# Second attention, first pass: the row maxima marked as high priority for VectorE's queue

## Chip, cores and metric

One NeuronCore of a Trainium2 chip. The metric is device microseconds for one execution of the whole program. The kernel before was timed three times: median 3221.76 us (3221.34 to 3221.77). One further execution was recorded by the hardware profiler.

## What is computed

The input x has 16 sequences of 512 tokens by 128 channels. Two gated layers follow each other, each of the form x + s(xn) * silu(g(xn)), with xn the layer norm of x. In the first, s is a gated causal convolution and g a two-layer transformer with local attention (8 heads of 64, windows of 64). In the second, s is attention over the whole sequence (16 heads of 8 channels) and g a soft mixture of experts. The change sits in the second layer's attention:

```
q = apply_rope(proj(Wq, bq), rope)
k = apply_rope(proj(Wk, bk), rope)
scores = jnp.einsum('bhqd,bhkd->bhqk', q, k) / math.sqrt(hd)
probs = jax.nn.softmax(scores, axis=-1)
out = jnp.einsum('bhqk,bhkd->bhqd', probs, v)
```

## The kernel before

**Stages.** The body is a set of Python generators, each of which emits the instructions of one stage for one of the 16 sequences ("batches"): C the convolution and P the setup (once each), L0 and L0b the two transformer layers (`layer`), A the start of the second layer (`pre`: gate, norm, q, k and v, rope, transposes), S1 and S2 the two passes of the second attention (`first`, `second`), M the mixture of experts (`moe`). A heap merges the generators: every `yield` tells how much work was just emitted, and PLAN gives each stage a start and a length in units of batches, so that some eight stages of several batches are emitted interleaved.

**Order of the queues.** That emission order is not yet the order of the instructions. It gives each instruction a priority, and Tile's scheduler, which plays the program through with times of its own, gives each engine in turn the instruction of best priority among those it holds ready. What comes out is one fixed list for each engine. In the trace an engine starts its instructions in that order, and stands idle when the next one lacks an input or a free buffer. `tc.high_priority()` puts the instructions traced inside it ahead of all others in this choice; the existing `tied` helper uses it to keep groups of matmuls together.

**S1 (`first`, L566 to L597).** For each batch there are four groups `G_` of four heads. A group loads packed queries QS and keys KS (three sets in turn, DMAs at L575 and L576), and then does 16 steps, four query tiles `qt` by four heads `g`:

```
sc = pt_("s1", "s1")
PE.matmul(sc, QS[:, g // 2, qt * 128 : qt * 128 + 128], KS[:, g % 2, :], start=True, stop=True)
V.tensor_reduce(mx[:, g, qt : qt + 1], sc, AX.X, ALU.max)
yield 0.7
```

So one step is a score matmul on TensorE (L583, tile s1c, one PSUM bank) and a maximum over its 512 keys on VectorE (L584, into one column of tile mw). There are 16 x 4 x 16 = 1024 steps, 64 to a batch. The tag s1 owns one PSUM bank, so the matmul of a step can start only when the maximum of the step before has read the bank; for the last two batches `TAIL` lets it use a second bank. After 16 steps mw is transposed (L587, tile pmc), negated and split (L589, L590), stored (L593) and written into spare rows of QS (L595), so that the second pass gets scores with the maximum already subtracted.

**S2 (`second`).** For each group 16 matmuls (L618, tile s2d, one bank), each followed by an exponential on ScalarE (L620); after each second key tile 8 matmuls with the values (L602, tile pvd), at the end a copy and four transposes. `turned` releases the QS and KS set.

**Others that this text names.** In `layer`: the projection into bank pq (L221 to L223 for the three parts of one product) is read by ScalarE (L335, L336) and by VectorE (L337, L341), then a sum of squares (L348, VectorE) and the normalisation on GpSimd; the scores of the local attention (L379) are masked and their minima taken on VectorE (L392, eight pairs of instructions to a window group), exponentials on ScalarE (L396), transposes (qT, kT, prT; they all carry L209), values (L123, L126), 1/sum and product (L414, L415), output projection (L433). In `moe`: logits (plb, also L221 to L223) with a maximum (L723), puob (L731, read at L732, L733, L736). At the end of `second`: the gate and residual (L657 to L662).

Of the kernel before, what the change touches and what calls it, by code (L numbers as in the profile page):

```python
# [13 lines left out]
ALU = mybir.AluOpType  # L14
AX = mybir.AxisListType
# [82 lines left out]
def body(ctx, tc, a):  # L98
    nc = tc.nc
    NB = a["x"].shape[0]  # L100
    V, S, G, PE = nc.vector, nc.scalar, nc.gpsimd, nc.tensor
# [90 lines left out]
    def mk(sid, b, dflt):  # L192
        def tl(shape, tag, dt=F32):
            cnt[0] += 1
            tg = f"{tag}{sid}"
            return pools[sid].tile(shape, dt, tag=tg, name=f"{tag}{sid}_{b}_{cnt[0]}", bufs=NBUF.get(tg, 2))

        def pt_(nm, tag=dflt):
            cnt[0] += 1
            alt = TAIL.get((tag, NB - b))  # L200
            if alt:
                turns_[tag] = turns_.get(tag, 0) + 1
                tag = alt[turns_[tag] % len(alt)]
            return psb.tile([128, 512], F32, tag=TAGS[tag], name=f"{nm}{sid}_{b}_{cnt[0]}", bufs=NPSUM[TAGS[tag]])

        def quad(src, nm, tag=dflt):
            pt = pt_(nm, tag)
            for p in range(4):
                PE.transpose(pt[:, p * 128 : p * 128 + 128], src(p), ident)  # L209
            return pt  # L210

        def split(pt, tag):
            t = tl([128, 2, 512], tag, F32R)
            S.copy(t[:, 0, :], pt)
            V.tensor_tensor(t[:, 1, :], pt, t[:, 0, :].bitcast(F32), ALU.subtract)  # L215
            return t

        return tl, pt_, quad, split
# [258 lines left out]
    def together(key, act, last=None):  # L477
        if key is None:
            act()
            return  # L480
        want = (0, 3)
        k = key[1]
        n = sum(0 <= k - o < NB for o in want)
        meet.setdefault(key, []).append((last is not None, act, last))
        if len(meet[key]) == n:
            todo = sorted(meet[key], key=lambda x: x[0])
            first = todo[0][1]()
            if todo[-1][2] is not None and len(todo) > 1:
                behind(first, todo[-1][2])
            tied([lambda: first] + [x[1] for x in todo[1:]])  # L490
            meet[key] = None
        while meet[key] is not None:
            yield 0.3
# [72 lines left out]
    def first(b):  # L566
        tl, pt_, quad, split = mk("c", b, "aS1")
        for G_ in range(4):
            n = 4 * b + G_
            assert turned[0] > n - len(ops)  # L570
            QS, KS = ops[n % len(ops)]
            qsrc = scq[b % 2, 128 * G_ : 128 * G_ + 128]
            ksrc = sck[b % 2, 128 * G_ : 128 * G_ + 128]
            for i in range(2):
                dma(out=QS[64 * i : 64 * i + 64, i, :].bitcast(F32), in_=qsrc[64 * i : 64 * i + 64].bitcast(F32))  # L575
                dma(out=KS[i:128:2, i, :].bitcast(F32), in_=ksrc[i:128:2].bitcast(F32))  # L576
            mw = maxima[n % 2]
            mx = mw[:, 0:16].rearrange("t (g q) -> t g q", g=4)
            yield 2
            for qt in range(4):  # L580
                for g in range(4):
                    sc = pt_("s1", "s1")
                    PE.matmul(sc, QS[:, g // 2, qt * 128 : qt * 128 + 128], KS[:, g % 2, :], start=True, stop=True)  # L583
                    V.tensor_reduce(mx[:, g, qt : qt + 1], sc, AX.X, ALU.max)  # L584
                    yield 0.7
            pm = pt_("pm")
            PE.transpose(pm[:80, 0:128], mw, ident)  # L587
            mm = tl([16, 2, 128], "mm", F32R)
            S.activation(mm[:, 0, :], pm[:16, 0:128], AF.Copy, scale=-1.0)  # L589
            V.scalar_tensor_tensor(mm[:, 1, :], pm[:16, 0:128], -1.0, mm[:, 0, :].bitcast(F32), ALU.mult, ALU.subtract)  # L590
            dst = mxd[b % 2, G_]
            for i in range(2):
                dma(out=dst[i].rearrange("j n t -> n j t").bitcast(F32), in_=mm[8 * i : 8 * i + 8].bitcast(F32))  # L593
            for i in range(2):
                dma(out=QS[64 * i + 48 : 64 * i + 52, i, :].bitcast(F32), in_=dst[i].rearrange("j (g q) t -> (j g) (q t)", g=2).bitcast(F32))  # L595
            qks[b, G_] = (QS, KS)
            yield 1  # L597
# [257 lines left out]
    def late():  # L855
# [81 lines left out]
    box, xrs, prs = {}, {}, {}  # L937
    make = {
        "L0": lambda b: layer(b, 0, box), "L0b": lambda b: layer(b, 1, box), "A": pre, "S1": first, "S2": second,
        "M": lambda b: moe(b, xrs, prs),  # L940
        "C": lambda b: conv(), "P": lambda b: setup(),
# [91 lines left out]
```

## Time and profile before

| | us |
|---|---|
| median of three runs | 3221.76 |
| profiled execution, its own time | 3220.23 |
| its span | 3218.4 |
| PE busy | 2932.7 (91%) |
| PEld busy | 2173.2 (68%) |
| DVE busy | 2334.5 (73%) |
| ACT busy | 2071.7 (64%) |
| POOL busy | 1596.0 (50%) |
| L584, 1024 maxima | 697.9 busy, 685 ns each |
| L583, 1024 score matmuls | 454.5 busy, 446 ns each |

PE is TensorE's matmuls, PEld its weight loads, which overlap them; DVE is VectorE, ACT ScalarE, POOL GpSimd and SP the engine that issues most DMAs. The span runs from the first to the last instruction of the profiled execution; 1.8 us of its time lie outside. A row of the waits says which instruction's engine stood idle, and which instruction's end let it go on, with the sum, the number of times and the longest. A row of the timeline gives the start in the span, the duration, the engine, the line, the operation and the tiles (out<-in), and in brackets the idle time before it. Line numbers are those of the kernel before; in the changed kernel the lines from the maximum on are one higher.

### The profile page before, as it was taken

The numbers are of one execution on the slowest core, as the hardware profiler recorded it, in microseconds if no ns is written. First come the engines' busy times: TensorE is split into PE (matmuls) and PEld (weight loads), VectorE is DVE, ScalarE is ACT, GpSimd is POOL, SyncE is SP. The second block draws the span as 40 slices with busy tenths as digits, with TensorE's granted clock in tenths as the row PEclk, the third lists the DMA queues.
The fourth block names the chain that finished last, engine by engine and source line by source line (L and its number), as shares of the span: only waits on it lengthen the run. The fifth ranks groups of instructions, "written<-read, shape, count | busy, mean of one in ns | idle before, by whom it ended". The sixth has DMA issues, their size and how long they took to land.

```text
span 3218.4 us, 67550 instructions
## 1 busy us (share of the span) xinstructions
PE 2932.7 (91%) x24164; PEld 2173.2 (68%) x24164; DVE 2334.5 (73%) x7165; ACT 2071.7 (64%) x4803; POOL 1596.0 (50%) x1854
## 2 busy tenths in 40 slices
PE   5798878889999999999999999999999999999897
PEld 4687756566767767676767677676767676666553
DVE  5779567768777877777787778777777778776563
ACT  2645445657766766676666667676766766656565
POOL 2424366655546473745556464747465564542200
PEclk7999979999999999999999999999999999999998
DMA  7555443122222222222222221221222222211110
GB/s 249 146 141 131 109 118 95 51 81 65 79 65 66 64 79 73 53 82 61 79 66 84 58 76 54 78 73 53 83 59 80 67 82 57 72 51 50 29 46 18
DMA packets 199549, 251.55 MB, mean 78 GB/s; under 512 B 57488, under 2 KB 123184, under 8 KB 199216
## 3 DMA queue, kind: packets, MB, share of 16 engines
q1 hardware_dynamic: 180784, 196.90, 21.4%
q0 software_dynamic: 18432, 50.34, 6.0%
q8 instruction: 193, 3.16, 0.4%
q14 instruction: 140, 1.15, 0.1%
HBM read 159.84 MB, written 57.50 MB: 68 GB/s over the span
## 4 chain that ended last, share of the span: by engine, by line
PE 57%; DVE 17%; ACT 13%; POOL 5%; issue 4%; DMA 3%; SPq 1%; POOLq 0%; DVEq 0%; ACTq 0%
PE pvd L602 7%; PE s2d L618 5%; PE s1c L583 5%; PE pw L433 3%; DVE mw L584 3%; ACT sd L620 3%; PE pw L471 3%; PE sc L379 2%; PE pq L221 2%; PE prT L209 2%; PE ppb L714 2%; DVE pr L392 2%; ACT pr L396 2%; PE pq L223 2%; PE pq L222 2%
## 5 line engine op out<-in xcount | busy, mean ns | idle before, releaser
L584 DVE TENSOR_REDUCE mw<-s1c 128x1 f32<-128x512 f32 x1024 | 697.9, 685 | 260.3 <-PE s1c L583 253.0
L620 ACT ACTIVATE sd<-s2d 128x512 f32<-128x512 f32 x1024 | 612.4, 603 | 331.5 <-PE s2d L618 325.2
L618 PE MATMUL s2d<-QS,KS 128*128 128x512 f32 x1024 | 479.6, 471 | 44.7 <-ACT sd L620 39.7
L583 PE MATMUL s1c<-KS,QS 128*128 128x512 f32 x1024 | 454.5, 446 | 51.8 <-DVE mw L584 43.5
L354 POOL TENSOR_TENSOR y<-ss,mhalf 128x8 f32<-128x8 f32 x256 | 429.6, 1678 | 15.6
L396 ACT ACTIVATE pr<-pr,m 128x128 f32<-128x128 f32 x1024 | 333.6, 396 | 107.9 <-DVE m L392 107.8
L352 POOL TENSOR_SCALAR ss<-ss 128x8 f32<-128x8 f32 x256 | 62.1, 242 | 641.8 <-DVE ss L348 621.7
L618 PEld LDWEIGHTS s2d<-QS,KS 128*128 128x128 f32 x1024 | 192.2, 188 | 237.7 <-issue 114.3
L350 POOL TENSOR_TENSOR rt<-rt,q 128x512 f32<-128x512 f32 x256 | 328.0, 1281 | 3.5 <-DVE q L341 3.5
L335 ACT ACTIVATE q<-pq 128x256 f32<-128x256 f32 x512 | 197.4, 385 | 143.7 <-PE pq L223 136.0
L355 POOL TENSOR_TENSOR rt<-rt,y 128x512 f32<-128x512 f32 x256 | 268.7, 1050 | 16.2
L583 PEld LDWEIGHTS s1c<-KS,QS 128*128 128x128 f32 x1024 | 193.6, 189 | 121.1 <-DVE mw L584 92.4
L337 DVE TENSOR_TENSOR rt<-pq,rot 128x256 f32<-128x256 f32 x512 | 212.4, 415 | 73.1 <-ACT vbuf L336 48.9
L602 PE MATMUL pvd<-sd,Vt 128*32 128x512 f32 x2048 | 249.2, 605 | 1.9 <-ACT sd L620 1.9
L221 PE MATMUL pq<-wq,hT 128*128 128x384 f32 x512 | 207.3, 405 | 25.1 <-DVE q L341 16.9
L341 DVE TENSOR_TENSOR q<-pq,rot 128x256 f32<-128x256 f32 x512 | 212.7, 415 | 0.0
L348 DVE TENSOR_REDUCE ss<-q 128x8 f32<-128x512 f32 x256 | 174.3, 681 | 50.8 <-ACT q L335 50.3
L209 PE MATMUL prT<-step,pr 128*128 128x128 f32 x1024 | 189.6, 281 | 15.3 <-ACT pr L396 10.5
L401 ACT COPY pt<-prT 128x512 f32<-128x512 f32 x256 | 152.3, 595 | 63.8 <-PE prT L209 61.1
L223 PE MATMUL pq<-wq,hT 128*128 128x384 f32 x512 | 178.6, 349 | 1.4 <-DVE hT L215 0.4
L323 POOL DMA_DIRECT2D wq<-wqd x128 | 81.4, 636 | 197.8 <-PE pq L223 140.4
L222 PE MATMUL pq<-wq,hT 128*128 128x384 f32 x512 | 178.8, 349 | 0.0
(255 smaller groups left out, 7435.9 us busy)
## 6 DMA issues: line engine op xcount, KB each, us to landing
wq<-wqd POOLq DMA_DIRECT2D x128, 384.0 KB, 3.7
w<-w1d SPq DMA_DIRECT2D x32, 682.0 KB
vsbuf<-vbuf SPq DMA_DIRECT2D x128, 130.0 KB
QS<-scq SPq DMA_DIRECT2D x128, 128.0 KB
KS<-sck SPq DMA_DIRECT2D x128, 128.0 KB
vsbuf<-vbuf SPq DMA_DIRECT2D x128, 97.5 KB
scq<-sa SPq DMA_DIRECT2D x96, 128.0 KB
sck<-sa SPq DMA_DIRECT2D x96, 128.0 KB
```

What stands on the lines that cost most here:

```text
L209: PE.transpose(pt[:, p * 128 : p * 128 + 128], src(p), ident)
L221: PE.matmul(out, lh, rh, start=start, stop=False)
L222: PE.matmul(out, lh, rl, start=False, stop=False)
L350: G.tensor_tensor(rf, rf, t2.rearrange("t p d -> t (p d)"), ALU.add)
L354: G.tensor_tensor(y.rearrange("t p g -> t (p g)"), sh, mhalf[:, 0:8], ALU.pow)
L355: G.tensor_tensor(rt[:, ps], rt[:, ps], y[:, :, :, None].to_broadcast([128, 2, 4, 64]), ALU.mult)
L396: S.activation(pr[:, hh, p, :], pr[:, hh, p, :], AF.Exp, bias=m[:, hh, p : p + 1], scale=-1.0)
L583: PE.matmul(sc, QS[:, g // 2, qt * 128 : qt * 128 + 128], KS[:, g % 2, :], start=True, stop=True)
L584: V.tensor_reduce(mx[:, g, qt : qt + 1], sc, AX.X, ALU.max)
L602: return PE.matmul(pv[32 * q : 32 * q + 32, :], Vt[:, kt, 9 * hd : 9 * hd + 32], e, start=(last == 1 and kt == 1), stop=(last == 3 and kt ...
L618: PE.matmul(sc, KS[:, g % 2, kt * 128 : kt * 128 + 128], QS[:, g // 2, :], start=True, stop=True)
L620: S.activation(e, sc, AF.Exp, scale=ISQ8)
```

## The change

The maximum of each step is traced inside `tc.high_priority()`. The matmul in front of it, the other stages, the buffers, PLAN and the yields are as they were.

```
                     PE.matmul(sc, QS[:, g // 2, qt * 128 : qt * 128 + 128], KS[:, g % 2, :], start=True, stop=True)
-                    V.tensor_reduce(mx[:, g, qt : qt + 1], sc, AX.X, ALU.max)
+                    with tc.high_priority():
+                        V.tensor_reduce(mx[:, g, qt : qt + 1], sc, AX.X, ALU.max)
                     yield 0.7
```

## Prediction

> **What bounds the kernel now.** I read the page's engine totals first, then the waits by engine, then the windows, then the timeline at the places where TensorE stops. The totals:
>
> ```profile
> PE 2932.7 (91%) x24164; PEld 2173.2 (68%) x24164; DVE 2334.5 (73%) x7165; ACT 2071.7 (64%) x4803; POOL 1596.0 (50%) x1854
> ```
>
> PE is busy for 2932.7 of 3218.4 us, so all its idle time is 285.7 us, and VectorE has 884 us to spare. The waits of PE over the whole span, then the top wait of VectorE:
>
> ```profile
> PE s1c L583 <- DVE mw L584: 43.5, 99, 1.6
> PE s2d L618 <- ACT sd L620: 39.7, 59, 2.7
> ...
> PE pq L221 <- DVE q L341: 16.9, 24, 4.5
> ```
>
> ```profile
> DVE mw L584 <- PE s1c L583: 253.0, 265, 3.9
> ```
>
> The change aims at the first row: a score matmul waits for the maximum before it to free the one bank. The row is 43.5 us, 1.4% of the span; that is the most the change can take away there. The last row says that 265 of the 1024 maxima had VectorE standing ready before their matmul ended: those can't come sooner by a better place in VectorE's queue.
>
> The windows tell the kernel's phases:
>
> ```profile
> 519.20:1252.70 733.50, 683.22 (x5847) 507.30 (x5848) 552.33 (x1768) 494.98 (x1172) 409.80 (x467) 0.99 0.25 71
> 1252.70:2662.90 1410.20, 1340.02 (x11297) 986.90 (x11296) 1077.56 (x3369) 981.16 (x2305) 781.12 (x897) 1.00 0.25 70
> 2662.90:3090.60 427.70, 393.08 (x2796) 268.30 (x2795) 292.00 (x805) 274.68 (x578) 159.66 (x196) 0.98 0.19 54
> 3090.60:3218.40 127.80, 107.80 (x558) 58.39 (x556) 55.04 (x113) 73.72 (x139) 9.93 (x13) 0.93 0.08 22
> ```
>
> The first PE figure is busy time. The second window is a steady state of eight batches: in the order of the queues each batch repeats the one before, instruction by instruction, every 176.3 us (1410.2 / 8). PE idles there for 70.2 us, 8.8 a batch. The waits of that window hold this row:
>
> ```profile
> PE s1c L583 <- DVE mw L584: 23.7, 56, 0.8
> ```
>
> 56 / 8 = 7 stalls a batch, always at the same steps, 2.96 us together. I number a batch's 64 steps from 0 and give, from the timeline (means of seven batches), the stall ahead of a step and, in brackets, how long the maximum of the step before had to wait after its matmul's end: 9: 0.37 (0.04), 23: 0.16 (0.55), 25: 0.36 (0.04), 33: 0.63 (2.18), 35: 0.24 (1.07), 48: 0.78 (0.04), 55: 0.42 (1.83). Three of them, 1.51 us, are pure latency: the maximum started 0.04 us after its matmul, took 0.69, and 0.05 later the next matmul ran. No order on VectorE helps these. The other four, 1.45 us a batch, stand behind other VectorE work: L348 (23), L662 (33), L392 (35 and 55).
>
> **The change, part by part.** It adds and removes no instruction: 1024 maxima at 685 ns remain. What moves is read from the orders of both programs side by side. *First*, in the steady state all of S1 moves ahead by two steps: the interval before step r + 2 now holds what the interval before step r held, for 50 of 64 intervals on PE and 51 of 64 on VectorE, identically. Without S1, 897 of 908 PE and 351 of 357 VectorE instructions of a batch keep their order. So the maxima don't leap out of VectorE's queue; they already were where the scheduler held them ready, and one place lets S1 squeeze in a step. I cost the shift by itself at nothing: the same PE work surrounds each of the seven stalls, which are now ahead of steps 11, 25, 27, 35, 37, 50 and 57. Step 33's maximum stays behind L662, and the L392 groups stay whole (111 unbroken runs before, 123 after). The transposes of mw (L587) and the DMAs to QS behind them stay beside the same PE work, so S2 starts no sooner. On SP the only steady change is that both stores into QS (L595) now precede the loads of A instead of standing around them. I cost that at nothing, since A has a batch's time.
>
> *Second*, the place itself, steps 52 to 61. Before, at step 55:
>
> ```profile
> 1754.66 0.29 DVE L392 CUSTOM_DVE_ANT_0 pr<-sc,maskf 128x128 f32<-128x128 f32 x1
> 1754.87 0.08 DVE L392 DVE_READ_ACCUMULATOR2_ANT m<- 128x1 f32 x1
> 1754.87 0.69 DVE L584 TENSOR_REDUCE mw<-s1c 128x1 f32<-128x512 f32 x1
> 1755.47 0.68 DVE L723 TENSOR_REDUCE mb<-plb 128x1 f32<-128x512 f32 x1
> 1756.07 0.42 DVE L337 TENSOR_TENSOR rt<-pq,rot 128x256 f32<-128x256 f32 x1
> 1756.40 0.42 DVE L341 TENSOR_TENSOR q<-pq,rot 128x256 f32<-128x256 f32 x1
> 1756.73 0.68 DVE L584 TENSOR_REDUCE mw<-s1c 128x1 f32<-128x512 f32 x1
> ```
>
> ```profile
> 1754.89 0.30 PE L209 MATMUL prT<-step,pr 128*128 128x128 f32 x1
> 1755.61 0.50 PE L583 MATMUL s1c<-KS,QS 128*128 128x512 f32 x1 [0.42 <-DVE mw L584]
> 1755.95 0.27 PE L209 MATMUL prT<-step,pr 128*128 128x128 f32 x1
> 1756.30 0.44 PE L209 MATMUL qT<-step,rt 128*128 128x128 f32 x2
> 1756.58 0.38 PE L209 MATMUL prT<-step,pr 128*128 128x128 f32 x2
> 1756.96 0.41 PE L221 MATMUL pq<-wq,hT 128*128 128x384 f32 x1
> ```
>
> The reader sees eight L392 pairs delay the maximum, PE stop for 0.42 us, and L723, L337, L341 follow. In the new order the maximum stands behind the same pairs (still ends at 1755.56), but the next one overtakes L337 and L341, and PE's list reads: score, five transposes, score, prT, s2d, pq, where it read score, five transposes, pq, s2d, score. The prT that ran at 1754.89 inside the stall moves behind it. The walk: PE reaches the second score at 1756.96; VectorE starts L723 at 1755.47 and the second maximum at max(1756.07, matmul end 1756.11 + 0.04) = 1756.15, ending at 1756.84; the bank is free at 1756.89. Covered by 0.07. L337 and L341 follow at 1756.75 and end at 1757.50, 0.68 later than before; PE reaches pq after score 0.23 (1757.80 to 1758.03), prT 0.15 and s2d 0.23 at 1757.57; its bank is free at 1757.55. Covered by 0.02. What is lost is the prT that the stall used to hide, about 0.15 us a batch. The row for this spacing is 1754.87 to 1755.47: a 0.69 maximum lets its successor start after 0.60.
>
> The Trainium skill speaks against this step: "VectorE: DVE Perf Modes", section "The DRAIN you can't avoid", says that the next operation does not start until the pipe is empty, though it lets an instruction that is not held start earlier. By the strict reading L341 would end some 0.3 us later and pq would wait 0.25 us a batch; the rows show overlap, so I don't use it.
>
> The new order repeats from the fourth batch on instead of the fifth; with the partly steady ones I count ten batches: 10 x 0.15 = 1.5 us. *Third*, outside the steady state. In the first batches PE's order differs in a few per cent of rows; I take nothing. From 2662.9 on, where L0, M and S2 run out, only about 0.6 of PE's rows keep their place. PE idles there 34.6 + 20.0 = 54.6 us (427.70 - 393.08 and 127.80 - 107.80); at the steady 5.0% it would be 27.7. The 27 us above that are chains that some other order fills better or worse; I let a quarter of it, 7 us, go either way, and take nothing, since the last matmuls of S1 and S2 keep their distance from the end (22.4 us of PE work before and 22.8 after for S1, 3.9 in both for S2).
>
> Sum: 3220.23 + 1.5 = 3221.7 us for an execution like the profiled one, which lies 1.53 below the median; so 3223.3 us for the median.
>
> **Rivals.** *Faster: the maxima do escape.* For: 1.45 us a batch stands behind other VectorE work. Against: the orders keep it there. Price if all of it came back: 10 x 1.45 = 14.5, so 3207 us. *Slower: bank pq.* At the place above L341 ends 0.68 us later and pq's cover is 0.02 us. It decides if PE reaches pq before 1757.55 on this scale, or if the second maximum is late, as its cover is 0.07. Price: 0.68 a batch if the wait is exposed once, 6.8 in all, and 13.6 if L348 and the GpSimd chain behind it make PE wait again for the transposes of rt: 3229 to 3236 us. For: pq already waits 16.9 us for L341. Against: 24 times only, and mostly outside the steady state. *The end.* The rearranged last batches give 7 us either way: 3216 or 3230. *That it does nothing it says* is nearly my forecast: the order hardly changes.
>
> **Chances.** Forecast, 3223 with 3217 to 3228 as its own range: 0.47. Maxima escape: 0.10. Bank pq: 0.25. The end: 0.10 for faster, 0.08 for slower. A measurement of this kernel tells about 0.2% (6.4 us) from no change. Faster 0.10 + 0.10 = 0.20; same 0.47; slower 0.25 + 0.08 = 0.33. The range takes in the end (3216) and pq's upper price (3236) and leaves out most of the escape, from 3210 down.
>
> **What would show it.** Right: in a middle batch still seven or eight stalls at L583, 2.5 to 3.5 us together, the L392 runs whole ahead of a maximum, a stall of about 0.57 us there, and the batch still 176 us. Wrong: the row L583 <- L584 in the steady window far below 23.7 us (escape), a new row pq <- L341 there of 0.3 us a batch or more (bank pq), or an equal steady window with a last stretch (556 us from the 13th batch's S1 on) that differs by over 5 us (the end).

## The result and the profile after

The changed kernel takes 3229.93 us (median of 20 runs, 3219.77 to 3237.3); the kernel before took 3223.16 us beside it (20 runs, 3212.08 to 3231.77). The ratio is 1.0021, 95% interval 1.0013 to 1.003: about 6.8 us slower, just over what can be told from no change. The forecast of 3223.3 was the kernel before's time; the result lies 6.6 us above it, outside the forecast's own range (up to 3228) and inside the whole one (up to 3236). One execution of the last experiment ran at a granted clock of 0.837 and took 3376 us; the ratios below leave it out.

The profiled execution of the changed kernel happened to be the fastest of its 20 (3219.77 us, span 3218.0, mean granted clock 0.977 against 0.974), so the two spans shown are nearly equal (3218.0 and 3218.4 us). The loss has to be read stage by stage, not from the spans.

The engine totals of the changed kernel:

```profile
PE 2930.9 (91%) x24164; PEld 2166.4 (67%) x24164; DVE 2336.3 (73%) x7165; ACT 2067.8 (64%) x4803; POOL 1595.1 (50%) x1854
```

The waits of PE in it (sum, times, longest):

```profile
PE s1c L583 <- DVE mw L585: 43.3, 96, 1.6
PE s2d L619 <- ACT sd L621: 38.6, 59, 2.9
...
PE pq L221 <- DVE q L341: 15.3, 20, 3.6
...
PE s1c L583 <- DMA KS<-sck: 6.5, 8, 2.4
```

The row that the change aims at went from 43.5 to 43.3 us, but that is a sum of opposite parts. Counted batch by batch in the two traces, it falls from 5.1 to 2.6 us in batch 0, rises from 31.2 to 33.9 in batches 1 to 11, and falls from 7.1 to 6.8 in the last four. In the steady state the maxima did not escape. In the steady window, of eight batches as before (1243.7 to 2653.5), the same row and that of bank pq:

```profile
PE s1c L583 <- DVE mw L585: 25.6, 56, 0.8
...
PE pq L221 <- DVE q L341: 1.8, 7, 0.3
```

Still 56 stalls, now 25.6 us instead of 23.7, which is +0.24 us a batch. The second row is in the kernel before with the same 1.8 us and 7 times, so bank pq is not the cause. The windows, each beginning at the same S1 step as before:

```profile
515.70:1243.70 728.00, 679.77 (x5793) 501.99 (x5794) 550.62 (x1749) 491.06 (x1166) 408.75 (x465) 0.99 0.26 71
1243.70:2653.50 1409.80, 1340.34 (x11297) 985.43 (x11296) 1077.21 (x3369) 978.96 (x2304) 780.50 (x896) 1.00 0.25 70
2653.50:3090.60 437.10, 399.38 (x2841) 271.71 (x2840) 294.57 (x823) 276.11 (x580) 160.50 (x197) 0.98 0.19 53
3090.60:3218.00 127.40, 106.81 (x568) 59.57 (x568) 56.17 (x114) 74.84 (x142) 9.90 (x13) 0.95 0.08 23
```

Length minus PE's busy time gives PE's idle time. It falls by 2.1 us in the first window (48.2 against 50.3), is level in the second (69.5 against 70.2, though the row above grew by 1.9 us there; PLACE below shows where its cost lies), and rises by 3.7 in the last two (37.7 + 20.6 = 58.3 against 34.6 + 20.0 = 54.6). The lengths of the first and third windows mislead: S1 reaches its steps two steps (5.5 us) earlier here, which shortens one (728.0 for 733.5) and lengthens the other (437.1 for 427.7).

### The profile page after: what moved, and what is told of

The parts are those of the page before. It is cut to its first block, busy times and chain, and to the rows that moved or that the text cites. A ratio compares the mean times of both kernels' runs of the same rounds, so it can differ in the third digit from the quotient of the medians.

```text
span 3218.0 us, 67606 instructions
## 1 busy us (share of the span) xinstructions
PE 2930.9 (91%) x24164; PEld 2166.4 (67%) x24164; DVE 2336.3 (73%) x7165; ACT 2067.8 (64%) x4803; POOL 1595.1 (50%) x1854
## 3 DMA queue, kind: packets, MB, share of 16 engines
q14 instruction: 140, 1.15, 0.1%
## 4 chain that ended last, share of the span: by engine, by line
PE 57%; DVE 17%; ACT 13%; issue 5%; POOL 4%; DMA 3%; SPq 1%; POOLq 0%; DVEq 0%; ACTq 0%
PE pvd L603 6%; PE s2d L619 6%; PE s1c L583 5%; PE pw L433 3%; DVE mw L585 3%; ACT sd L621 3%; PE pw L471 3%; DVE pr L392 3%; PE prT L209 2%; PE sc L379 2%; PE pq L221 2%; PE ppb L715 2%; ACT pr L396 2%; PE pslb L693 2%; PE pq L223 2%
## 5 line engine op out<-in xcount | busy, mean ns | idle before, releaser
L583 PE MATMUL s1c<-KS,QS 128*128 128x512 f32 x1024 | 454.9, 446 | 53.1 <-DVE mw L585 43.3
L337 DVE TENSOR_TENSOR rt<-pq,rot 128x256 f32<-128x256 f32 x512 | 211.7, 414 | 63.3 <-ACT vbuf L336 57.9
L341 DVE TENSOR_TENSOR q<-pq,rot 128x256 f32<-128x256 f32 x512 | 211.5, 413 | 0.0
```

## Experiments

Three parts could carry the loss, and the orders of the queues allow each to be had nearly alone, by giving the priority to some batches only. PLACE: the one place in a steady batch, 0.24 us each. LEAD, its rival: the two steps by which S1 runs ahead cost by themselves. END: the rearranged last batches. START: the first batches. CHANCE: the difference is a draw of the granted clock. The edit is always to the line `with tc.high_priority():` ahead of the maximum, where `ExitStack()` does nothing. All runs are timed beside the kernel before on the same chip: 3218.62 us (33 runs) for the first four, 3219.02 (27) for the next four, 3221.02 (23) for the last two. The medians of before differ by 2.4 us among these chips, so only ratios are set against each other.

### Batches 0 to 11, batches 12 to 15, and none that matter

```diff
-                    with tc.high_priority():
+                    with (tc.high_priority() if b < NB - 4 else ExitStack()):
```

> Priority for the maxima of batches 0 to 11 only. The order of the queues is then that of the changed kernel up to the 13th batch's scores and that of the kernel before at the end (the last batch identical). Theory END (the loss of some 7 us lies in the last four batches, whose order the change shuffles): within 3 us of before, ratio 0.999 to 1.001, and the stretch from the 13th batch's S1 on as long as before's, apart from the two steps of lead. Rival STEADY (the loss is 0.15 us and a pq wait in each of ten batches): slower by 5 to 7 us, ratio 1.0015 to 1.0022, and the steady batch 0.5 to 0.7 us longer than 176.3.

Measured: 3223.19 us, ratio 1.0012 (1.0002 to 1.0022).

```diff
+                    with (tc.high_priority() if b >= NB - 4 else ExitStack()):
```

> Priority for the maxima of batches 12 to 15 only. The order is that of the kernel before up to batch 12 and that of the changed kernel in the last two batches. END: slower by 5 to 9 us, ratio 1.0015 to 1.003, with the stretch between the 14th and 15th batch's S1 about 5 us longer (155 instead of 150) and its PE waits of s2d for ScalarE doubled. STEADY: within 2 us of before.

Measured: 3221.58 us, ratio 1.0013 (1.0003 to 1.0023).

```diff
+                    with (tc.high_priority() if b >= NB - 2 else ExitStack()):
```

> Priority for the maxima of the last two batches only. All queues have the same order as in the kernel before, so this is the control: both theories say ratio 1.000. If it differs from 1 by more than 0.001, the difference of 0.21% between the two kernels can't be told from chance or from the placing of code, and neither theory is needed (rival CHANCE).

Measured: 3218.9 us, ratio 0.9996 (0.9986 to 1.0007). With the last two batches alone marked, no queue's order differs from before, and the time doesn't either.

The changed kernel once more, with no edit:

> The changed kernel once more, on the same chip as the three others. END and STEADY: ratio 1.0013 to 1.003 as before. CHANCE: anything from 0.999 to 1.003. If END holds, its time is head's plus tail's excess.

Measured: 3228.17 us, ratio 1.0029 (1.0018 to 1.0039). What follows: the loss is real and comes again, and a program with the old orders shows none. The mean granted clock of the runs is nearly the same here for the changed kernel (0.9753) and the one before (0.9751). So CHANCE falls. Head and tail lose 3.9 and 4.2 us, 8.1 together, about the whole (6.8 and 9.3 in its two measurements); each has an interval of some 3 us either way, so the sum is no sharp test. Neither theory met its numbers: END wanted 0.999 to 1.001 for the head and 1.0015 to 1.003 for the tail, STEADY 1.0015 to 1.0022 for the head and a tail within 2 us of before. Both parts lose.

### Batches 4 to 11: PLACE without the lead

```diff
+                    with (tc.high_priority() if 4 <= b < 12 else ExitStack()):
```

> Priority for the maxima of batches 4 to 11 only. S1 does not get its two steps of lead; the order differs from before's by the one place in those eight batches (98% of the rows equal) and nowhere else. Theory PLACE (the steady loss is the stall at that one place): batches 5 to 11 each 0.2 to 0.3 us longer than before's at the same granted clock (175.2 becomes 175.4 to 175.5, 176.8 becomes 177.0 to 177.1), the stall ahead of step 55 0.6 to 0.7 us instead of 0.42, the whole 2 us slower, ratio 1.000 to 1.001. Rival LEAD (the two-step shift itself costs): batches as long as before's.

Measured: 3221.26 us, ratio 1.0002 (0.9993 to 1.0011). The whole loss of 8 x 0.24 = 1.9 us lies inside that interval, as does none; the trace decides. The first batches keep the old order here, so S1 has no lead, and six of the seven stalls of a batch stand at the old steps with the old lengths. The seventh, at step 55, is 0.66 us instead of 0.42. From the timeline of PE in this kernel, one such batch:

```profile
1754.39 0.50 PE L583 MATMUL s1c<-KS,QS 128*128 128x512 f32 x1 [0.66 <-DVE mw L585]
```

Its steady batches take at least 175.5 us where the granted clock is 1.00 and 177.1 where it is 0.99; those of before 175.2 and 176.8. At the same clock single batches of either kernel are up to 0.7 us longer, so the shortest are compared, first before, then here:

```profile
1252.74:1427.98 175.24, 166.67 (x1414) 122.72 (x1412) 134.40 (x422) 122.64 (x289) 97.52 (x113) 1.00 0.26 70
1428.02:1603.50 175.48, 166.86 (x1414) 122.73 (x1412) 134.40 (x422) 122.47 (x289) 97.76 (x113) 1.00 0.25 70
```

The shortest batch of the changed kernel, which has the lead, takes 175.47 us. So the lead costs nothing in the steady state, and the place costs 0.24 to 0.29 us a batch, to be seen only where the clock is the same. PE's idle time in these batches is the same (8.57 us before, 8.62 here, 8.57 in the changed kernel): the cost is PE's busy time.

### Batch 13 alone: END

```diff
+                    with (tc.high_priority() if b == 13 else ExitStack()):
```

> Priority for the 64 maxima of batch 13 only. Steady state as before, the end in the changed kernel's order. END: 4 to 6 us slower, ratio 1.001 to 1.002; from the 13th batch's middle to the end about 392.5 us instead of 388, PE idle there 42 to 43.5 us instead of 40. If it is as fast as before, the end needs the other batches' maxima as well.

Measured: 3226.22 us, ratio 1.0021 (1.0012 to 1.003). The priority of 64 maxima, after thirteen batches in the old order, loses as much as all 1024, a little more than the 4 to 6 us expected. The lists of PE, VectorE, ScalarE and GpSimd in this kernel's trace are, instruction by instruction, those of the kernel that marks batches 12 to 15. So the two are one schedule measured twice, 1.0013 and 1.0021, and the priority of batches 12, 14 and 15 changes nothing there. PE's idle time between S1's first step of batch 13 and that of batch 15, summed from each trace, parts the kernels cleanly:

| kernel | batch 13 | batch 14 | sum, us |
|---|---|---|---|
| before | 12.8 | 13.3 | 26.1 |
| batches 4 to 11 | 13.1 | 12.3 | 25.4 |
| batches 0 to 11 | 12.8 | 14.2 | 27.0 |
| changed | 17.1 | 12.2 | 29.3 |
| changed, again | 17.0 | 11.8 | 28.8 |
| batches 12 to 15 | 16.8 | 11.9 | 28.6 |
| batch 13 alone | 16.8 | 12.0 | 28.8 |

The four other kernels with the old end have sums of 24.9 to 25.9 us. So the rearranged end adds some 3 us of idle time. From where S2 is at step 36 of batch 12 to the end of the span it adds 5 us in all: that stretch takes 391.5 to 394.1 us in the four traces that have it (mean 392.9) and 386.2 to 389.7 in the seven that have the old end (before, and the kernels that mark batches 14 and 15, 4 to 11, 0 to 11, 0 and 1 (twice), or 0; mean 387.7). Of these 5.2 us, 3.2 are PE's idle time and 2.0 its busy time. The granted clock doesn't explain them: its mean there is 0.965 in the four and 0.963 in the seven. Which waits grew: those of PE from 2828 us on in the kernel before, and from 2820 on in the changed one:

```profile
PE s2d L618 <- ACT sd L620: 12.9, 27, 2.7
...
PE ppb L714 <- ACT Db L707: 4.5, 3, 2.3
PE s1c L583 <- DMA KS<-sck: 2.2, 3, 1.3
```

```profile
PE s2d L619 <- ACT sd L621: 12.8, 28, 2.9
PE ppb L715 <- ACT Db L708: 5.4, 3, 2.7
...
PE s1c L583 <- DMA KS<-sck: 4.2, 7, 1.1
```

S2's wait for its exponentials, the largest row, is the same. S1's wait for the keys grew by 2.0 us and M's wait for its activation by 0.9; the rest is rows under 1 us. Both rows part all eleven traces: the keys cost 3.1 to 4.2 us in the four with the new end and 1.3 to 2.4 in the seven others, M's activation 5.4 to 5.5 and 4.5 to 4.7. About 1 us of it stands at one place, S1's first step of batch 14, in the kernel before and in the changed one:

```profile
2978.70 0.40 PE L583 MATMUL s1c<-KS,QS 128*128 128x512 f32 x1
```

```profile
2976.70 0.47 PE L583 MATMUL s1c<-KS,QS 128*128 128x512 f32 x1 [1.15 <-DMA KS<-sck]
```

The second load of its keys is issued 4.9 us ahead of that step before, and 0.8 us ahead of it in the changed kernel. The four traces wait 0.95 to 1.15 us here, the seven not at all. There is no single culprit: another order of the same work fills the last chains a little worse. Why the scheduler's order of the end comes out so isn't settled by these runs.

### Batches 0 and 1, batch 0 alone: START

```diff
+                    with (tc.high_priority() if b < 2 else ExitStack()):
```

> Priority for the maxima of batches 0 and 1 only. The order falls back to before's in batch 2. PLACE and END: ratio 1.000 within 0.001. Rival START (something lost ahead of the steady state): slower by 2 us or more.

Measured: 3215.56 us, ratio 0.9986 (0.9976 to 0.9997): faster than both kernels, which neither expectation allowed. From batch 3 on the orders are those of before, so the gain sits in the first batches. The waits of PE from 510 to 720 us, which holds S1's batch 0, in the kernel before and in this one:

```profile
PE s1c L583 <- DVE mw L584: 5.1, 10, 1.6
```

```profile
PE s1c L583 <- DVE mw L585: 2.5, 5, 1.6
```

And in the changed kernel, in the same stretch:

```profile
PE s1c L583 <- DVE mw L585: 2.6, 5, 1.6
```

Here the maxima do escape: six stalls of 0.24 to 0.78 us (at steps 33, 43, 44, 48, 60 and 61) are gone, one of 0.39 is new. To tell whether batch 0 is enough, and whether the gain returns:

```diff
+                    with (tc.high_priority() if b < 1 else ExitStack()):
```

> High priority for the maxima of batch 0 alone; the orders of all queues are those of before from batch 1 on, and batch 0 is ordered as in the kernel with the first two. START theory (the gain of the first two batches is the 2.5 us of stalls that batch 0 loses): ratio 0.9990 to 0.9993, TensorE's idle time in batch 0 at 27 us against 29.4, the row s1c <- mw of 510 to 720 us at 2.5 us against 5.1. Rival CHANCE (the first two were faster by a draw of the granted clock): ratio 1.000 within 0.0005, whatever the rows.

Measured: 3219.35 us, ratio 0.9992 (0.998 to 1.0004).

> The kernel with the first two batches once more, on the same chip as the one with the first alone. START: ratio 0.9986 to 0.9993, and no better than batch 0 alone, since batch 1 showed no idle time gained (5.9 us against 6.0). Rival (batch 1 gains too, by the order alone): better than batch 0 alone by 0.0004 or more. CHANCE: 1.000 within 0.0005.

Measured: 3218.54 us, ratio 0.9989 (0.9978 to 1.0). The rows are as START has them: the wait for mw in that stretch is 2.6 us in both, and PE's idle time in batch 0, with the wait for its first keys, is 27.9 and 27.3 us, and was 27.0 in the first measurement, against 29.4. Without that wait, from S1's first step of batch 0 to that of batch 1, PE idles for 24.6 to 25.4 us in the six traces in which batch 0 is marked, and for 26.8 to 27.9 us in the five in which it isn't: about 2.1 us less. All three ratios lie below 1; the two later intervals touch it. Of the 3.5 us of the first measurement a part is the clock, whose mean over the runs was 0.9762 against 0.9748 before; in the two later ones it was lower than before's (0.9747 and 0.9748 against 0.9755), and they were faster all the same. Of a gain of 2 us no single comparison of times here is certain; the rows and the idle time are. Batch 1, marked, shows only the stall of the place (0.66 us for 0.42) and the same idle time (5.9 us against 6.0); whether it adds anything to the time stays open (0.9989 and 0.9986 against 0.9992).

### The score matmul in the priority as well

```diff
-                    PE.matmul(sc, QS[:, g // 2, qt * 128 : qt * 128 + 128], KS[:, g % 2, :], start=True, stop=True)
                     with tc.high_priority():
+                        PE.matmul(sc, QS[:, g // 2, qt * 128 : qt * 128 + 128], KS[:, g % 2, :], start=True, stop=True)
                         V.tensor_reduce(mx[:, g, qt : qt + 1], sc, AX.X, ALU.max)
```

> High priority for the score matmul as well as for its maximum, in all batches. TensorE's list then takes S1's matmul as soon as the scheduler holds the bank free. Theory PE LIST (where the next score stands in TensorE's list sets the stalls, not the place of the maximum in VectorE's): the row of score matmuls waiting for maxima changes clearly from 43 us, and as each matmul now stands right behind the end of a maximum that the chip finishes later than the scheduler holds, it grows, to 60 us or more, and the kernel is 10 to 40 us slower (ratio 1.003 to 1.012). Rival VECTORE LIST: S1 comes out of the way early and the row falls below 30 us; ratio 0.995 to 0.999.

Measured: 3306.78 us (4 runs), ratio 1.0262 (1.0243 to 1.0281). The waits of PE in it:

```profile
PE s2d L619 <- ACT sd L621: 65.2, 102, 2.4
...
PE s1c L584 <- DMA KS<-sck: 17.2, 28, 2.2
PE s1c L584 <- DVE mw L585: 15.5, 44, 1.6
```

Both expectations were wrong, though the rival had the row right (below 30 us). The row that the change aimed at fell from 43.5 to 15.5 us, and the kernel lost 2.6%: S2 now waits 65.2 us for its exponentials (39.7 before) and S1 17.2 us for keys (4.5 before). A steady batch takes 180.7 to 182.5 us instead of 175 to 177, with 11 to 12.6 us of idle time instead of 8.6. The idle time explains about half of that; the other half is PE busy longer with the same 24164 matmuls (2974.1 us against 2932.7). The granted clock is lower as well, 0.970 against 0.974; in proportion that would be some 12 of these 41 us, an estimate. Why the rest is busy longer isn't shown.

## Why the prediction was right or wrong, point by point

**The steady state's shift, right.** The seven stalls are at steps 11, 25, 27, 35, 37, 50 and 57, as named, six of them unchanged within 0.01 us (0.37, 0.17, 0.35, 0.63, 0.24, 0.78). S1's shift and the stores on SP cost nothing in the steady state: the clock-matched batch is 0.2 to 0.3 us longer than before's with the shift and without it.

**The place, right in kind, mis-sized: 0.15 forecast, 0.24 measured.** PE's timeline there in the changed kernel:

```profile
1753.79 0.50 PE L583 MATMUL s1c<-KS,QS 128*128 128x512 f32 x1 [0.66 <-DVE mw L585]
...
1755.07 0.51 PE L583 MATMUL s1c<-KS,QS 128*128 128x512 f32 x1
1755.41 0.27 PE L209 MATMUL prT<-step,pr 128*128 128x128 f32 x1
1755.58 0.50 PE L619 MATMUL s2d<-QS,KS 128*128 128x512 f32 x1
1755.91 0.34 PE L221 MATMUL pq<-wq,hT 128*128 128x384 f32 x1
...
1756.45 0.60 PE L209 MATMUL plTb<-step,sb 128*128 128x128 f32 x4
```

VectorE beside it:

```profile
1753.05 0.69 DVE L585 TENSOR_REDUCE mw<-s1c 128x1 f32<-128x512 f32 x1
1753.65 0.68 DVE L724 TENSOR_REDUCE mb<-plb 128x1 f32<-128x512 f32 x1
1754.32 0.69 DVE L585 TENSOR_REDUCE mw<-s1c 128x1 f32<-128x512 f32 x1
1754.93 0.41 DVE L337 TENSOR_TENSOR rt<-pq,rot 128x256 f32<-128x256 f32 x1
1755.26 0.41 DVE L341 TENSOR_TENSOR q<-pq,rot 128x256 f32<-128x256 f32 x1
```

The order is the one walked through, and the stall is 0.66 (0.57 forecast). From the end of the delayed maximum to the start of plTb, by when the same work is done, the changed kernel takes 1756.45 - 1753.74 = 2.71 us, the kernel before 1758.03 - 1755.56 = 2.47. The term that failed is the price of matmuls in the new order. I gave the second score and s2d 0.23 us each, the spacing they had when they followed one another. With a transpose between them they take 0.34 and 0.33, and the prT 0.17 for my 0.15: 0.84 where I had 0.61. The three parts of pq give 0.07 back (0.54 for 0.61), as do the transposes ahead (1.28 for 1.35). The price stood in the lines that the prediction shows: the score at 1755.61, behind a transpose, lets its successor start at 1755.95, after 0.34. The stall's own growth, 0.24 us as well, isn't this cost: it lies ahead of the walk's start, and PE's idle time in a batch didn't grow (8.57 us in both kernels). The longer stall stands in eleven batches, 1 to 11, where the prediction counted ten: 11 x 0.24 = 2.6 us for 1.5.

**Bank pq, rightly only a rival, and dead.** L341 ends at 1755.67 and pq starts at 1755.91, so the cover is 0.2 us and not 0.02: the later score and s2d gave it that time. The wait row is 1.8 us in both kernels.

**The DRAIN rule of the Trainium skill ("VectorE: DVE Perf Modes", section "The DRAIN you can't avoid"), rightly not used.** In the new order L724 starts 0.60 after the maximum's start and L337 0.61 after the next one's, each of 0.69. The prediction priced the strict reading at a wait of pq of 0.25 us a batch on its own cover of 0.02; on the cover of 0.2 that there is, it would be under 0.1, an estimate. So the unchanged row of pq alone doesn't decide it; the overlap in these rows does.

**"In the first batches I take nothing", wrong.** A few per cent of PE's rows sufficed to take six of ten stalls from S1 in batch 0 and add one: 2.5 us of the row, 2.1 us of idle time. The rival "the maxima do escape" was right there, and there alone; I had priced it on the steady state, where the order had settled.

**The end, taken as nothing between -7 and +7, is the bulk.** It costs about 5 us, inside the bound, on the side that I gave 0.08. The step that failed: the argument that S1's and S2's last matmuls keep their distance from the end says nothing about the chains between, where PE's idle time rose by 3.2 us and its busy time by 2.0. (In the traces PE is busy for 30.7 us after S1's last matmul before and for 29.7 in the changed kernel, and for 5.8 us after S2's in both, which are not the prediction's 22.4, 22.8 and 3.9; that the distances hardly move is right.) Batch 13 alone shows the same idle time with one batch marked. The sign that the prediction named, a last stretch that differs by over 5 us, has to be cleared of the lead first: 564.5 us against 555.5 is 9.0, of which 5.5 are the lead, so 3.5 remain.

**The sum.** Start about -2, place 11 x 0.24 = +2.6, end +5: between 5 and 6 us. In the first measurement the medians differ by 6.8 with an interval of 4.2 to 9.7, in the second the ratio gives 9.3 with 5.8 to 12.6. The sum is within the first and at the edge of the second, so 1 to 4 us could be missing. The first twelve batches alone measured +3.9 (0.6 to 7.1), where start and place by themselves make +0.6. That remainder is not explained; that kernel's trace shows some 1.5 us more idle time in batches 13 and 14 than the six others with the old end (27.0 against a mean of 25.4). There S1 gives its two steps of lead back: its lists differ from before's up to 3029 us. Forecast: +1.5, because one part with the right sign was too small and two of opposite sign were set to nothing. That these two partly cancel, and that the whole range holds the result, is luck: the range reached to 3236 for bank pq, which played no part, and to 3230 for the end, which had 0.08.

## What to carry to other kernels

A priority in a static scheduler changes the lists, and a list that repeats is read once: compare the orders, find the place that differs, walk it, and multiply by the batches; but price start and end as parts of their own, where few instructions of another order decide. Here the priority paid in batch 0 alone; marking the first two batches alone gave 0.9986 and 0.9989 while marking all gave 1.0021. A smaller wait row is no gain in itself: the row fell by 28 us and the kernel lost 88.

## What the runs showed of the hardware

- The granted clock moves by amounts small enough to hide such a change: one steady batch takes 175.2 us at 1.00 and 176.8 at 0.99, in the same program and the same execution. That is five times or more what the place costs.
- S1's batch 0 ran at a granted clock between 0.945 and 0.982 in the profiled executions, and took 191.2 to 196.1 us. The whole program spreads by 17 to 20 us over 20 runs.
- The spacing of the 128x512 score matmuls (s1c, s2d) goes by what runs ahead of them: in the steady window of the kernel before, the next matmul starts 0.23 us after one that stands behind another 128x512, and 0.32 us after one that stands behind a 128x128, whether a 128x512 or a 128x128 follows (medians). At the place it was 0.33 to 0.34 us.
